# Mixture-of-experts loop of a fused graph and feed-forward kernel: the first-layer third piece loaded a step ahead in two halves, and a PSUM tile for each column half

## The chip, the core and the metric

The kernel runs on one NeuronCore of a Trainium2 chip. The metric is the device time of one execution in microseconds. The names of the engines are those of the profile: PE is TensorE (PEld its weight loads), DVE VectorE, ACT ScalarE, POOL GpSimd, SP SyncE, which in this kernel only issues transfers.

## What is computed

The program is one layer of a graph attention network over 625 nodes and 20,000 edges, followed by a transformer block with a mixture of experts. The change lies in the last part alone. In the reference that part reads:

```python
h2 = _ln(x, ln2_g, ln2_b).reshape(-1, d)                  # 625 rows of d = 768
gate_logits = h2 @ Wg                                     # 8 experts
w, sel = jax.lax.top_k(gate_logits, K)                    # K = 1
w = jax.nn.softmax(w.astype(jnp.float32), axis=-1)        # one chosen expert: weight 1
...
hid = jax.nn.relu(jnp.einsum('nd,edf->enf', h2, W1) + b1[:, None, :])   # 3072 wide
y = jnp.einsum('enf,efd->end', hid, W2) + b2[:, None, :]
moe = jnp.einsum('ne,end->nd', combine, y)
return x + moe.reshape(b, t, d)
```

With K = 1 each row goes through one expert, so the kernel sorts the rows by expert and runs each expert over its own rows only. All weights are float32. An expert has W1 of 768 x 3072 and W2 of 3072 x 768, each 9.4 MB.

## The kernel before

**Stages.** The graph layers and the attention come first. During the attention's last tiles the routing picks an expert for each row (`choose`), finds the row's place (`send`) and scatters the rows, sorted by expert, into the DRAM buffers `xg` (normed rows) and `xr` (residual rows, with the row's number in an extra column). Then the experts run.

**Steps.** A `step` takes up to 128 rows of one expert. The first one, `step_a`, takes 128 rows of the expert with the most rows; it is traced before the loop, since its expert is known early. All others run in a hardware loop (`For_i`, L1354) of as many iterations as the routing found. An expert's rows are cut into at most one block of 32, one of 64 and then blocks of 128; the loop's body holds an arm for each of the three sizes (L1370 to L1376), and a word of `table` tells the iteration its size, its expert, the next step's expert, and whether that one is new. An expert with several blocks keeps its weights.

**Weights.** An expert's weights stand in six SBUF tiles: `w1[0..2]`, each 1024 of the 3072 hidden columns of W1, and `w2[0..2]`, each 1024 of the hidden rows of W2. There is one copy of each. A piece is loaded as two transfers of 1536 KB, called halves here (`load_piece`; `load_half` is the one W2 half). `load_expert`, called behind each step, puts the next expert's loads into SP's queue in the order `w1[0]`, `w1[1]`, `w1[2]`, the second bias `b2b`, `w2[0]`, `w2[1]`, `w2[2]`; SP keeps that order (a manual schedule), and each load waits until the running step has read the tile it goes to. If the next step has the same expert, the transfers are switched off by `cond`. The last half of `w2[2]` takes another way: it is loaded into the tile `ahead` at the start of the step before (`load_ahead`, L1362), and ScalarE copies it into place at the start of its own step (L1361).

**Inside a step.** `into(c)` multiplies the rows with a block of W1 into the PSUM tile `ph`, and VectorE copies it to `hb` (L1102). `turn(c)` transposes `hb` on PE into `tp` (L1109), and ScalarE adds the first bias and applies Relu into `hbT` (L1114). `out_of(c)` multiplies `hbT` with a block of W2 and adds up in `py` (L1122), a PSUM tile with one bank for each half of the 768 columns. There are three blocks c at 32 and 64 rows, where P = 4 or 2 column groups of PE work side by side, and six at 128 rows. PE's order is written by hand; in the loop it is

```python
for c in range(2, n):
    turn(c - 2)
    into(c)
turn(n - 2)
out_of(0)
turn(n - 1)
for c in range(1, n):
    if c > n - 3:
        turned = turn_rows(xbT, xb, sp, c + 2 - n, nc.scalar.copy)
    out_of(c)
```

after `into(0)` and `into(1)`. `turn_rows` transposes the next step's rows in two parts (L892), which ScalarE copies to `xbT` (L893); its PSUM buffers are the two of `tp`. The last `out_of` does its products sorted by column half. Behind it VectorE adds the sums to `yo` in eight instructions (L1175), and POOL scatters `yo` into the output (L1177). ScalarE, VectorE and POOL have no order by hand: the planner of the framework places them.

## Time and profile before

| | |
|---|---|
| median of 3 runs | 1071.32 us (1071.0 to 1073.14) |
| the profiled execution | 1073.13 us, its span 1071.0 us |
| mean granted TensorE clock | 0.987 |
| bytes of SP's hardware queue | 175.57 MB |
| step 0 (before the loop) ends | 702.1 us |
| loop steps: rows, and start in the span | 64: 702.1; 128: 738.0; 64: 805.5; 32: 839.8; 128: 867.7; 64: 933.1; 32: 967.3; 64: 995.4; 32: 1029.7 |
| last product of the last step ends | 1057.6 us |

The profile is of one execution, and all its times are in us from the start of its span. The 2 us between its span and its own time lie outside what the trace shows. A line such as L1122 is a line of the listing above. A group "py<-ew,hbT" names the output and the inputs by tile; all of the experts' weight tiles are called `ew` there. float32 products appear as two records each. A mark in brackets at a line's end says how long the engine was idle before, and what released it. "SPq" is SP's queue: a line there is the issue of a transfer, not its duration. In the view by stretches the columns are, for each engine, busy us and (instructions), then the granted clock as a share of full speed, the busy share of the 16 DMA engines, and GB/s.

By the transfer rates in the steps, weights are fetched for the steps that start at 805.5, 839.8, 933.1, 967.3 and 1029.7; the other loop steps go on with the expert that is there.

### The profile page before, as it was taken

The numbers are of one execution on the slowest core, as the hardware profiler recorded it, in microseconds if no ns is written. First come the engines' busy times: TensorE is split into PE (matmuls) and PEld (weight loads), VectorE is DVE, ScalarE is ACT, GpSimd is POOL, SyncE is SP. The second block draws the span as 40 slices with busy tenths as digits, with TensorE's granted clock in tenths as the row PEclk, the third lists the DMA queues.
The fourth block names the chain that finished last, engine by engine and source line by source line (L and its number), as shares of the span: only waits on it lengthen the run. The fifth ranks groups of instructions, "written<-read, shape, count | busy, mean of one in ns | idle before, by whom it ended". The sixth has DMA issues, their size and how long they took to land.

```text
span 1071.0 us, 14972 instructions
## 1 busy us (share of the span) xinstructions
PE 1006.0 (94%) x4763; PEld 576.6 (54%) x4764; DVE 456.4 (43%) x1306; ACT 344.3 (32%) x826; POOL 57.1 (5%) x97
## 2 busy tenths in 40 slices
PE   6889999999999999999999999999999899997993
PEld 4455456677656556666665655544463435543341
DVE  6886696385293920665537554011101121011211
ACT  6667544362130111444435211121202222122230
POOL 1200100000000100000001102000000000000000
PEclk9999999999999999999999999999999999999997
DMA  9300400300410357998001669212798969799693
GB/s 279 135 1 1 160 30 0 133 1 17 99 32 1 83 139 171 409 390 326 1 2 42 254 234 352 88 39 98 298 321 324 400 240 347 266 379 398 241 401 130
DMA packets 85928, 194.40 MB, mean 182 GB/s; under 512 B 32413, under 2 KB 34084, under 8 KB 85865
## 3 DMA queue, kind: packets, MB, share of 16 engines
q1 hardware_dynamic: 80345, 175.57, 46.0%
q0 software_dynamic: 5440, 17.86, 4.8%
q8 instruction: 36, 0.59, 0.2%
q10 hardware_dynamic: 80, 0.16, 0.1%
q14 instruction: 27, 0.22, 0.1%
HBM read 250.30 MB, written 38.37 MB: 270 GB/s over the span
## 4 chain that ended last, share of the span: by engine, by line
PE 66%; DVE 6%; DMA 6%; issue 4%; SPq 3%; ACT 1%; POOL 1%; POOLq 0%; DVEq 0%; ACTq 0%
PE py L1122 14%; PE ph L1098 14%; PE pq L809 7%; PE agg L529 6%; DMA ew<-in_L_ffn_W_dram 6%; PE ph L591 5%; PE ph L629 3%; PE pv L772 3%; PE ph L166 3%; SPq L1030 3%; PE sc L829 2%; PE o L870 2%; PE po L901 2%; PE tpe L852 1%; PE tph L1109 1%
## 5 line engine op out<-in xcount | busy, mean ns | idle before, releaser
L1122 PE MATMUL py<-ew,hbT 128*64 128x384 f32 (+2 forms) x960 | 192.7, 503 | 14.7 <-DMA ew<-in_L_ffn_W_dram 14.7
L1098 PE MATMUL ph<-ew,xbT 128*32 128x256 f32 (+2 forms) x864 | 153.4, 497 | 8.7 <-DVE bT L1067 4.8
L1122 PEld LDWEIGHTS py<-ew,hbT 128*64 128x64 f32 (+2 forms) x960 | 92.3, 147 | 96.5 <-issue 60.4
L1114 ACT ACTIVATE hbT<-tph,bT 128x64 f32<-128x64 f32 (+2 forms) x240 | 55.5, 334 | 198.4 <-PE tph L1109 121.3
L1098 PEld LDWEIGHTS ph<-ew,xbT 128*32 128x32 f32 (+2 forms) x864 | 62.8, 135 | 88.7 <-issue 81.5
L1175 DVE TENSOR_TENSOR yo<-yo,py 64x192 f32<-64x192 f32 (+2 forms) x80 | 27.3, 378 | 182.0 <-PE py L1122 180.9
L1102 DVE COPY hb<-ph 128x512 f32<-128x512 f32 (+1 forms) x39 | 24.5, 629 | 144.5 <-PE ph L1098 144.3
L529 PE MATMUL agg<-xl,zT 125*125 125x256 f32 (+1 forms) x300 | 79.8, 417 | 1.3 <-ACT zT L518 1.1
L529 PEld LDWEIGHTS agg<-xl,zT 125*125 125x125 f32 x300 | 54.5, 188 | 19.6 <-ACT zT L518 2.6
L356 PE MATMUL pp<-w,yT 128*125 128x512 f32 x120 | 57.0, 614 | 0.0
L231 ACT ACTIVATE step<-iota,past 125x314 f16<-125x314 f16 x120 | 55.9, 547 | 0.0
L629 PE MATMUL ph<-wr,h1T 128*125 128x384 f32 x160 | 52.8, 486 | 0.0
L591 PE MATMUL ph<-w,h1T 128*125 128x384 f32 x160 | 52.4, 486 | 0.0
L838 ACT ACTIVATE e<-e,nm 125x125 f32<-125x125 f32 (+4 forms) x60 | 36.0, 602 | 39.5 <-DVE nm L835 39.4
L248 PE MATMUL cps<-step,oh 125*125 125x314 f16 x181 | 38.0, 315 | 10.5 <-ACT step L231 5.4
L901 PE MATMUL po<-wpj,aT 128*125 128x384 f32 x120 | 44.3, 499 | 1.2 <-DVE nm L835 0.7
L241 DVE TENSOR_SCALAR oh<-iota,drel,upper 125x125 f16<-125x125 f16 x160 | 41.4, 316 | 4.0 <-PE cps L248 4.0
L166 PE MATMUL ph<-wr,yT 128*125 128x512 f32 x96 | 42.1, 593 | 0.1
L591 PEld LDWEIGHTS ph<-w,h1T 128*125 128x125 f32 x160 | 30.0, 188 | 21.1 <-issue 0.5
L248 PEld LDWEIGHTS <-oh 125*125 125x125 f16 x181 | 26.1, 147 | 28.2 <-DVE oh L241 13.9
L629 PEld LDWEIGHTS ph<-wr,h1T 128*125 128x125 f32 x160 | 29.8, 188 | 20.8
L809 PE MATMUL pq<-hT,L_ffn_Wq 128*128 128x313 f32 (+1 forms) x144 | 41.0, 432 | 0.0
(331 smaller groups left out, 1281.6 us busy)
## 6 DMA issues: line engine op xcount, KB each, us to landing
ew<-in_L_ffn_W_dram SPq DMA_DIRECT2D x122, 1536.0 KB
xr<-zt SPq DMA_DIRECT2D x5, 3076.0 KB
xg<-zt SPq DMA_DIRECT2D x5, 3072.0 KB
ahead<-in_L_ffn_W_dram SPq DMA_DIRECT2D x10, 1536.0 KB
w<-in_L_gnn_W_dram SPq DMA_DIRECT2D x4, 1536.0 KB
wr<-in_L_gnn_Wr_dram SPq DMA_DIRECT2D x4, 1536.0 KB
b2b<-in_L_ffn_b_dram SPq DMA_DIRECT2D x11, 384.0 KB
xb<-xg POOLq DMA_DIRECT2D x10, 384.0 KB, 6.4
```

The costliest lines, as they stand in the source:

```text
L166: nc.tensor.matmul(pp[:R, :], yT[:, c, cols(t)], part(wr1, KD, c, i, 512), start=(c == 0), stop=(c == KD - 1))
L231: nc.scalar.activation(o, iota[:, :SH + 1], AF.Sign, bias=at, scale=-1.0)
L248: nc.tensor.matmul(where, target(R, d[:, j:j + 1], w[:, j:j + 1]), step(s[:, j:j + 1], j % 4 != 3), start=False, stop=False, skip_group_ch ...
L356: nc.tensor.matmul(pp[:R, :], yT[:, c, cols(t)], part(w1, KD, c, i, 512), start=(c == 0), stop=(c == KD - 1))
L529: nc.tensor.matmul(self.agg[:R, c0:c0 + n], zT[:, s, :], xl[:, s, x0:x0 + n], start=(s == 0), stop=(s == T - 1))
L591: nc.tensor.matmul(ph[:R, :384], h1T[:, c, cols(t)], part(w2, KH, c, i, 384), start=(c == 0), stop=(c == KH - 1))
L629: nc.tensor.matmul(ph[:R, :384], h1T[:, k, cols(t)], part(wr2, KH, k, i, 384), start=(k == 0), stop=(k == KH - 1))
L809: nc.tensor.matmul(pp[:, :b - a], w[:, c, c0:c0 + 128], hT[:, c, a:b], start=(c == 0), stop=(c == KD - 1))
L901: mm = nc.tensor.matmul(pp[:R, i, :384], aT[:, c, cols(t)], wpj[i][:, c, :], start=(c == 0), stop=(c == KD - 1))
L1098: mm = nc.tensor.matmul(ph[g * M:(g + 1) * M, :C], xT[:, k, :M], w[:, k, o + g * C:o + (g + 1) * C], start=(k == 0), stop=(k == KD - 1))
L1114: nc.scalar.activation(hbT[c][:, k, r], tp[:, k, r], AF.Relu, bias=bT[:, f:f + 1])
L1122: mm = nc.tensor.matmul(py[g * M:(g + 1) * M, i, :384], hbT[c][:, k, g * M:(g + 1) * M], w[:, o + g * K + k, i * 384:(i + 1) * 384], start ...
```

## The change

- **What is loaded ahead.** No longer the last half of `w2[2]`, but both halves of `w1[2]`. Two buffers of three 1024-column blocks hold them: `ahead[0]` takes the place of the old `ahead`, and `ahead[1]` lies in the tile `xid`, which is allocated on all 128 partitions now and whose rows are no longer needed by then. `w2[2]` is loaded whole, in its turn.
- **When.** `load_expert` in step i loads, for step i + 1, `w1[0]`, `w1[1]`, `b2b`, `w2[0]`, then `w1[2]` of step i + 2 into `ahead`, then `w2[1]` and `w2[2]`. The call before the loop still loads all three `w1` pieces. The table's words get four more bits, the expert of the step after next and whether it is new.
- **Copies.** ScalarE copies `ahead[0]` into `w1[2]` after the last `into` of a step, and `ahead[1]` after the last `turn` (in program order). The copy at a step's start is gone.
- **Sums.** `py` becomes two tiles of one bank each, `py0` and `py1`.
- **Order.** `begun` is yielded outside of the manual PE schedule.

```diff
--- before.py
+++ after.py
@@ -74,7 +74,8 @@
     xg = dram.tile([NR, D], F32, name="xg")
     xr = dram.tile([NR, D + 1], F32, name="xr")
 
-    xid = keep.tile([R, T, D + 1], F32, name="xid")
+    xid_all = keep.tile([128, T, D + 1], F32, name="xid")
+    xid = xid_all[:R]
     x = xid[:, :, :D]
     bT_all = keep.tile([128, E * NK], F32, name="bT_all")
     nc.gpsimd.iota(xid.bitcast(I32)[:, :, D:D + 1].rearrange("p t o -> p (t o)"),
@@ -1027,20 +1028,19 @@
                                        name=f"ew{l}_{c}")
 
     def load_half(to, e, c, k, **cond):
-        nc.sync.dma_start(to, W2[ds(e, 1), c * FC + k * 128:c * FC + (k + 4) * 128, :]
-                          .rearrange("o (k p) d -> p (o k) d", p=128), **cond)
+        nc.sync.dma_start(to, W1[ds(e, 1), k * 128:(k + 3) * 128, c * FC:(c + 1) * FC]
+                          .rearrange("o (k p) f -> p (o k) f", p=128), **cond)
 
     def load_piece(e, l, c, **cond):
         if l:
-
-            for k in range(0, FC // 128 - (4 if cond and c == NFC - 1 else 0), 4):
-                load_half(w2[c][:, k:k + 4, :], e, c, k, **cond)
+            for k in range(0, FC // 128, 4):
+                nc.sync.dma_start(
+                    w2[c][:, k:k + 4, :],
+                    W2[ds(e, 1), c * FC + k * 128:c * FC + (k + 4) * 128, :]
+                    .rearrange("o (k p) d -> p (o k) d", p=128), **cond)
         else:
             for k in range(0, KD, 3):
-                nc.sync.dma_start(
-                    w1[c][:, k:k + 3, :],
-                    W1[ds(e, 1), k * 128:(k + 3) * 128, c * FC:(c + 1) * FC]
-                    .rearrange("o (k p) f -> p (o k) f", p=128), **cond)
+                load_half(w1[c][:, k:k + 3, :], e, c, k, **cond)
 
     def load_bias(e, **cond):
         nc.sync.dma_start(b2b, b2[ds(e, 1), :].to_broadcast([B, D]), **cond)
@@ -1066,18 +1066,24 @@
         of_e = bT_all.rearrange("p (e k) -> p e k", k=NK)[:, ds(e, 1), :]
         return bT, nc.vector.tensor_copy(bT, of_e.rearrange("p o k -> p (o k)"))
 
-    def load_expert(e, new):
+    def load_expert(e, new, later, last=NFC - 1):
 
 
         with tc.manual_schedule(engines={SP}):
-            for l in range(2):
-                for c in range(NFC):
-                    load_piece(e, l, c, cond=new)
-                if not l:
-                    load_bias(e, cond=new)
-
-    def load_ahead(e, **cond):
-        load_half(ahead, e, NFC - 1, FC // 128 - 4, **cond)
+            for c in range(last):
+                load_piece(e, 0, c, cond=new)
+            load_bias(e, cond=new)
+            load_piece(e, 1, 0, cond=new)
+            load_ahead(*later)
+            for c in range(1, NFC):
+                load_piece(e, 1, c, cond=new)
+
+    def load_ahead(e, new=None):
+        for i in range(2):
+            load_half(ahead[i], e, NFC - 1, 3 * i, **({} if new is None else dict(cond=new)))
+
+    def from_ahead(i):
+        nc.scalar.copy(w1[NFC - 1][:, 3 * i:3 * i + 3, :], ahead[i])
 
     def step(M, xT, bT, rb, after=None):
 
@@ -1087,7 +1093,7 @@
         C = 512 if P == 1 else FC // P
         n = DF // (C * P)
         K = C // 128
-        py = sp.tile([128, 2, 512], F32, name="py", bufs=1)
+        py = [sp.tile([128, 512], F32, name=f"py{i}", bufs=1) for i in range(2)]
         hb, hbT, copied = {}, {}, []
 
         def into(c):
@@ -1120,14 +1126,15 @@
             for k, i in sorted(order, key=lambda o: o[1]) if c == n - 1 else order:
                 for g in range(P):
                     mm = nc.tensor.matmul(
-                        py[g * M:(g + 1) * M, i, :384], hbT[c][:, k, g * M:(g + 1) * M],
+                        py[i][g * M:(g + 1) * M, :384], hbT[c][:, k, g * M:(g + 1) * M],
                         w[:, o + g * K + k, i * 384:(i + 1) * 384],
                         start=(c == 0 and k == 0), stop=(c == n - 1 and k == K - 1))
             return mm
 
         with tc.manual_schedule(engines={PE}):
             into(0)
-            yield into(1)
+            begun = into(1)
+        yield begun
         if after is None:
             with tc.manual_schedule(engines={PE}):
                 turn(0)
@@ -1152,9 +1159,11 @@
                 for c in range(2, n):
                     turn(c - 2)
                     into(c)
+                from_ahead(0)
                 turn(n - 2)
                 out_of(0)
                 turn(n - 1)
+                from_ahead(1)
                 for c in range(1, n):
                     if c > n - 3:
                         turned = turn_rows(xbT, xb, sp, c + 2 - n, nc.scalar.copy)
@@ -1172,7 +1181,7 @@
             for g in range(P):
                 for cc in range(4 // P):
                     cs = slice(cc * w, (cc + 1) * w)
-                    nc.vector.tensor_add(yv[:, i, cs], yv[:, i, cs], py[g * M:(g + 1) * M, i, cs])
+                    nc.vector.tensor_add(yv[:, i, cs], yv[:, i, cs], py[i][g * M:(g + 1) * M, cs])
 
         s = nc.gpsimd.indirect_dma_start(
             out=out, out_offset=bass.IndirectOffsetOnAxis(ap=idx[:M], axis=0),
@@ -1318,6 +1327,7 @@
     w = tabf[:, 2, :NS]
     v.scalar_tensor_tensor(w, a[:, 1:], 4.0, w, op0=OP.mult, op1=OP.add)
     v.scalar_tensor_tensor(w, a[:, :NS], 64.0, w, op0=OP.mult, op1=OP.add)
+    v.scalar_tensor_tensor(w[:, :NS - 1], a[:, 2:], 1024.0, w[:, :NS - 1], op0=OP.mult, op1=OP.add)
     v.tensor_copy(table, tabf[:, 2:, :])
     rt.close()
 
@@ -1331,17 +1341,17 @@
     first_rows = nc.gpsimd.dma_start(xb, xg[ds(row_0, B), :])
     first_turned, = step_a
     right.close()
-    ahead = ctx.enter_context(tc.tile_pool(name="ahp", bufs=1, reuse_waits="tile")).tile(
-        [128, 4, D], F32, name="ahead")
+
+    ahp = ctx.enter_context(tc.tile_pool(name="ahp", bufs=1, reuse_waits="tile"))
+    ahead = [ahp.tile([128, 3, FC], F32, name="ahead"),
+             xid_all.rearrange("p t d -> p (t d)")[:, :3 * FC].rearrange("p (k f) -> p k f", k=3)]
 
     def word(i, *engines):
-        return nc.values_load(table[0:1, 0, ds(i, 1)], min_val=0, max_val=1023,
+        return nc.values_load(table[0:1, 0, ds(i, 1)], min_val=0, max_val=16383,
                               **(dict(engines=engines) if engines else {}))
 
     word_0 = word(0, SP)
-    with tc.manual_schedule(engines={SP}):
-        load_ahead((word_0 >> 7) & 7)
-    load_expert((word_0 >> 7) & 7, (word_0 >> 6) & 1)
+    load_expert((word_0 >> 7) & 7, (word_0 >> 6) & 1, ((word_0 >> 3) & 7,), NFC)
 
     def all_of(step, *of):
         with tc.manual_schedule(engines={PE}):
@@ -1353,13 +1363,11 @@
     sp_order.close()
     with tc.For_i(0, n_blk, 1, iteration_sync="reg_based") as i:
         w = word(i)
-        kind, then = w & 3, ((w >> 3) & 7, (w >> 2) & 1)
+        kind, then = w & 3, ((w >> 3) & 7, (w >> 2) & 1, ((w >> 11) & 7, (w >> 10) & 1))
         row, row_next = (nc.values_load(table[0:1, 1, ds(k, 1)], engines=[pool], min_val=0,
                                         max_val=NR - B) for k in (i, i + 1))
 
         nc.gpsimd.dma_start(xb, xg[ds(row_next, B), :])
-        nc.scalar.copy(w2[NFC - 1][:, FC // 128 - 4:, :], ahead)
-        load_ahead(then[0], cond=then[1])
         bT, s = biases((w >> 7) & 7)
         tc.add_manual_dep(s.ins, first_rows.ins.name, ORDER)
```

## The prediction

> **What bounds the kernel now.** I read the page first (busy shares, the slices), then busy time by stretch, one stretch for each step of the expert loop, then PE's timeline in one narrow step, then SyncE's queue and ScalarE in that step. The page names TensorE, and the last slices say that the DMA engines are busy too:

> ```profile
> PE 1006.0 (94%) x4763; PEld 576.6 (54%) x4764; DVE 456.4 (43%) x1306; ACT 344.3 (32%) x826; POOL 57.1 (5%) x97
> ...
> DMA  9300400300410357998001669212798969799693
> ```

> An average of 94% does not say in which stage the rest is lost. The view by stretches does. I cut the loop at its steps (starts of `yo`'s sums): 64, 128, 64, 32, 128, 64, 32, 64, 32 rows, called steps 1 to 9. The rows below are steps 3 to 7 and 9:

> ```profile
> core 0: us, PE busy (x) PEld busy (x) DVE busy (x) ACT busy (x) POOL busy (x), PEclk, DMA share, GB/s
> 805.50:839.80 34.30, 34.30 (x187) 13.50 (x186) 4.58 (x14) 8.86 (x27) 2.12 (x3) 1.00 0.92 343
> 839.80:867.70 27.90, 20.72 (x253) 10.58 (x253) 4.85 (x14) 8.21 (x27) 2.05 (x3) 0.94 0.87 336
> 867.70:933.10 65.40, 65.40 (x203) 34.78 (x202) 9.71 (x17) 10.57 (x27) 2.04 (x3) 1.00 0.83 305
> 933.10:967.30 34.20, 34.20 (x190) 13.46 (x190) 4.57 (x14) 8.86 (x27) 2.13 (x3) 1.00 0.91 343
> 967.30:995.40 28.10, 21.77 (x256) 10.30 (x254) 5.02 (x14) 8.22 (x27) 2.06 (x3) 0.94 0.86 330
> ...
> 1029.70:1057.60 27.90, 21.59 (x253) 10.00 (x252) 5.03 (x15) 8.22 (x27) 2.04 (x3) 0.94 0.85 329
> ```

> 64- and 128-row steps are full of matmuls. The three 32-row steps (4, 7, 9) are not: PE is idle 6 to 7 us in each, the granted clock drops to 0.94, and the DMA engines run through. Steps 4, 7 and 9 are the ones whose expert is loaded during a step of only 34 us. PE's timeline of step 7:

> ```profile
> 976.16 0.84 PE L1122 MATMUL py<-ew,hbT 128*32 128x384 f32 x4
> 979.40 2.89 PE L1122 MATMUL py<-ew,hbT 128*32 128x384 f32 x28 [2.41 <-DMA ew<-in_L_ffn_W_dram]
> 982.23 0.44 PE L1109 MATMUL tph<-ident,hb 128*128 128x128 f32 x2
> 982.50 0.60 PE L892 MATMUL tpx<-ident,xb 128*128 128x128 f32 x4
> 983.81 0.84 PE L1122 MATMUL py<-ew,hbT 128*32 128x384 f32 x4 [0.71 <-DMA ew<-in_L_ffn_W_dram]
> 987.74 4.46 PE L1122 MATMUL py<-ew,hbT 128*32 128x384 f32 x28 [3.09 <-DMA ew<-in_L_ffn_W_dram]
> 992.14 0.44 PE L892 MATMUL tpx<-ident,xb 128*128 128x128 f32 x2
> 992.51 2.79 PE L1122 MATMUL py<-ew,hbT 128*32 128x384 f32 x32
> ```

> The second-layer products wait for the second weights, half piece by half piece, 3.93 us apart (983.81 to 987.74: 1536 KB at 400 GB/s). An undisturbed `out_of` takes 2.79 us (last line); the one after the 3.09 us wait takes 4.46 for its last 28 matmuls alone. So the narrow step is bound by transfers, and the queue that feeds them starts here:

> ```profile
> 936.07 0.38 SPq L1030 DMA_DIRECT2D ahead<-in_L_ffn_W_dram  x1
> 937.67 14.30 SPq L1040 DMA_DIRECT2D ew<-in_L_ffn_W_dram  x6
> ...
> 956.29 18.28 SPq L1030 DMA_DIRECT2D ew<-in_L_ffn_W_dram  x5
> ```

> Twelve halves and `b2b` for step 7 go out in step 6, none before 936.07.

> **The change part by part.**

> What goes. Between 936.07 and the last landing (987.74 + 3.93 = 991.7) lie 12 halves; the change leaves 10, since the third first-layer piece has been loaded a step earlier. Step 7 without waits, added from its own starts: 967.27 to 976.16 is 8.89; then `out_of(0)` 2.79, turn and row turn 0.87, `out_of(1)` 2.79, row turn 0.37, `out_of(2)` 2.87: 18.58 us. It takes 28.1, so 9.5 is lost. Step 9 (1029.63 to 1057.60, 27.97) loses 9.4. Step 4 starts its matmuls at 844.60, 4.81 after the step before, and then takes 23.07; 1.68 of that is its first two `into` at a clock of 0.56 (7.07 against 5.39). Its weights cost 23.07 - 18.58 - 1.68 = 2.8. Together **21.7 us** hang on the weights.

> [...] This stretch follows the 3.09 us wait:

> ```profile
> 987.70:989.70 2.00, 1.96 (x17) 0.92 (x21) 0.00 (x0) 0.00 (x0) 0.00 (x0) 0.67 1.03 402
> ```

> [...] The granted clock shows the drop, so I count it as regained.

> Do the ten halves land in time? Step 6: the tail of step 6's own weights (now with two halves for step 7 ahead of them) should run to about 939.9; four halves, `b2b`, `xb` and `rb` (7.27 MB, 18.2 us) end at 958.1. The first second-layer piece can't be issued before `out_of(0)` of step 6 frees it (956.29, PE's time, unchanged). Six halves and the next rows then take 24.8: the last lands at **982.9**. Step 7 wants it at 984.0 (with the stall below): 1.1 us to spare. Step 9 has no such tail (step 8 reloads nothing): 1043.5 against 1046.4. Step 4: about 855 against 863. A late landing costs us for us in steps 7 and 9, more if the clock drops.

> What comes. The one ScalarE copy at a step's start (2.75 us) becomes two in mid-step, in all nine steps, new expert or not. In before they stand like this:

> ```profile
> 967.57 2.76 ACT L1361 COPY ew<-ahead 128x3072 f32<-128x3072 f32 x1 [5.05 <-PE py L1122]
> ...
> 976.35 1.54 ACT L1114 ACTIVATE hbT<-tph,bT 128x32 f32<-128x32 f32 x8 [1.50 <-PE tph L1109]
> ```

> At a step's start nothing urgent is queued behind the copy. In mid-step, the first copy waits for the last `into`, and behind it stand the Relus of `turn(n-2)`, for which `turn_rows` (it takes that PSUM buffer) and `out_of(1)` wait. The trace of before has no Relu held up by the copy. [...] Bounds: 0, and 2.2 where the planner also puts the second copy ahead of the last Relus; I take 1.05, since the same row gives both durations, three times: **3.1 us**. [...]

> SyncE. `load_ahead` moves behind the first second-layer piece, ahead of four halves. It waits for the second copy (about 960 in step 6), and behind it `w2[1]` waits for PE until 961.2 anyway. If that copy came only at the step's end, four halves from 968 would land by 986: 2 us late. The skipped loads of a repeated expert still walk the queue; their issue took 0.07 us. Steps 2 and 5 load 12 halves in 65 us and have room (share 0.83). The extra half before the loop lies beside step 0, where PE is full and the DMA share 0.57. POOL's transfers only see fewer bytes beside them.

> The `py` halves. The eight sums of a 32-row step take 4.62 us after the last product:

> ```profile
> 1057.60 4.62 DVE L1175 TENSOR_TENSOR yo<-yo,py 32x384 f32<-32x384 f32 x8 [13.32 <-PE py L1122]
> ```

> The last `out_of` does column half 0 first, so four sums (2.3) can begin half of 2.79 earlier. Only the last step has its sums on the chain: **1.4 us** gained; elsewhere the next step hides them. One more table instruction on VectorE: 0.09 by its twin beside it, on the chain. Leaving the manual order before `begun` lets the planner place the small routing matmuls: -1 to +1.5, taken as 0. The pauses at the first run of each arm (1.57, 2.24, 4.81; none at a repeat) stay; the bounds are 3 less and 1 more.

> Sum: 21.7 - 3.1 + 1.4 - 0.1 = **19.9 us**. The profiled execution took 1073.13 (span 1071.0), 1.8 above the median of 1071.32: 1053.2 in its terms, 1051.4 as a median.

> **The rivals.**

> New waits take a part back (16%): the last halves land 1 to 4 us late in steps 7 and 9, or copies and Relus stand in the worse order. For it: spare time of only 1.1 us. Against: even the late case above misses by 2. Twice 1 to 4, plus up to 3.5 of ScalarE: 1054 to 1063.

> No change (4%): the halves that remain are held by the release of second-layer buffers, so the last one lands as late as before. The release at 967.3 plus two halves (978) speaks against it. 1070 to 1073.

> Slower (10%): ScalarE becomes the bound in mid-step. Both copies stand ahead of the Relus on which every `out_of` waits, and PE sits through them in all nine steps: 5.5 x 9 = 49.5 against 23 gained, about 1098. It decides from 2.5 us of stall per step on average. Against it: ScalarE is busy 8 to 11 us of a step, and the wide steps have 5 us of product in between.

> As forecast (70%): 1046 to 1056.

> **How the numbers follow.** About 0.2% (2 us) is what a measurement of this kernel can tell from none. Predicted 1051.5, the likeliest case. The range 1045.5 to 1061 takes in the bounds (3.1 if no Relu is held, 3 at first runs, on the low side; late halves and copies above) and most of the first rival; the other two and its tail, 2 in 10, are outside. Faster: 0.70 + 0.16 = 0.86; same 0.04; slower 0.10.

> **What would show it.** Right: steps 7 and 9 last 19 to 21 us with no wait of `py` for `ew` over 1 us and a granted clock of 1.00; step 4 ends 1.5 to 2.5 us sooner; 64- and 128-row steps keep 34.3 and 65.4; the second-layer issues end sooner after a step starts; the last sums end about 3.2 after the last product. Wrong: `tpx` or `py` waiting over 2 us for `hbT`, 64-row steps longer than 35 us, or the waits for `ew` still at 3 us.

## The result, and the profile after

The changed kernel takes **1063.18 us** (median of 4 runs, 1062.57 to 1065.18) against 1071.16 (4 runs, 1069.79 to 1073.14): a ratio of 0.9927, 95% interval 0.9907 to 0.9948. It is faster by 5.6 to 10 us, where 20 were forecast. A second series of the same program, on another chip, gave 1061.67 and a ratio of 0.9905 (0.9885 to 0.9925). The profiled execution took 1062.57 us (span 1060.6). It is the quickest of its runs and that of before was the slowest of its own, so the two traces lie 10.4 us apart and the medians 8.

The page of the changed kernel, its row of engines:

```profile
PE 1003.9 (95%) x4763; PEld 571.8 (54%) x4764; DVE 456.6 (43%) x1307; ACT 366.6 (35%) x835; POOL 57.1 (5%) x97
```

ScalarE has 22 us more to do in nine more instructions, one copy more in each step, and PE's own sum is nearly what it was. The view by stretches, cut at the same steps as in the prediction (here 2, 4, 6, 7 and 9; same columns):

```profile
735.50:807.40 71.90, 68.06 (x200) 35.83 (x200) 7.24 (x17) 13.10 (x28) 2.08 (x3) 0.95 0.65 238
...
841.70:865.10 23.40, 19.15 (x253) 8.84 (x253) 4.99 (x13) 10.75 (x28) 2.04 (x3) 1.00 0.81 311
...
930.40:964.70 34.30, 34.30 (x191) 13.58 (x194) 5.16 (x14) 11.39 (x28) 2.13 (x3) 1.00 1.03 399
964.70:988.30 23.60, 20.58 (x254) 9.11 (x255) 5.20 (x13) 10.65 (x28) 2.05 (x3) 0.93 0.84 312
...
1022.60:1048.90 26.30, 21.52 (x252) 9.49 (x251) 5.42 (x13) 10.74 (x28) 2.05 (x3) 0.94 0.77 298
```

Step 6 keeps its 34.3 us, so the copies in mid-step hold nothing there. Step 7 falls from 28.1 to 23.6, which is far from 18.6, and its clock is still 0.93. Step 9 falls by 1.4 only, and step 4 does not fall at all. Step 2 (71.9 with its pause) has a clock of 0.95. The DMA engines carry 399 GB/s all through step 6 (busy share 1.03) and yet 311 in step 4 (0.81). PE's timeline of step 7 shows what is left of the waits:

```profile
976.99 2.79 PE L1128 MATMUL py<-ew,hbT 128*32 128x384 f32 x32
979.71 0.44 PE L893 MATMUL tpx<-ident,xb 128*128 128x128 f32 x2
980.14 0.84 PE L1128 MATMUL py<-ew,hbT 128*32 128x384 f32 x4
984.00 4.31 PE L1128 MATMUL py<-ew,hbT 128*32 128x384 f32 x28 [3.02 <-DMA ew<-in_L_ffn_W_dram]
```

The first two waits of before (2.41 and 0.71) are gone. A third of the same length is left (3.09 there), but two halves further on: in before it was for the second half of `w2[1]`, here it is for the last half of `w2[2]`. After it the 28 products take 4.31 instead of 2.8. From the two traces, step by step (start of a step's first product to that of the next), in us:

| part | before | after | difference |
|---|---|---|---|
| all up to step 1's first product | 703.59 | 701.13 | -2.5 |
| step 1, with the pause at its end | 36.56 | 38.21 | +1.7 |
| step 2 | 65.3 | 68.0 | +2.7 |
| step 3, with the pause at its end | 39.1 | 34.2 | -4.9 |
| step 4: weights +2.0, slow start -1.7 | 23.07 | 23.37 | +0.3 |
| step 7 | 28.1 | 23.6 | -4.5 |
| step 9, to its last product | 27.8 | 26.4 | -1.4 |
| after the last product | 13.55 | 11.7 | -1.9 |

Steps 5, 6 and 8 are equal within 0.1. The weights, steps 4, 7 and 9 together, gave **3.9 us of the 21.7**. A second profile of the same program divides it otherwise (step 4 lasts 25.3, step 7 23.7, step 9 24.7) but comes to nearly the same, 3.7. The rest of the difference is pauses (-2.2 with their slow starts), sums (-1.9), and work before the loop (-2.5). I don't give the last to the change: `step_a` begins at 629.15 in this trace and at 628.22 in the second series of the same program, and in all eleven profiles of this study somewhere from 628.0 to 631.2.

The new wait has its root in SP's queue in step 2, in which everything for step 3 and the `ahead` of step 4 goes out:

```profile
776.62 0.35 SPq L1046 DMA_DIRECT2D b2b<-in_L_ffn_b_dram  x1
780.68 5.97 SPq L1037 DMA_DIRECT2D ew<-in_L_ffn_W_dram  x2
787.25 0.37 SPq L1031 DMA_DIRECT2D ahead<-in_L_ffn_W_dram  x1
788.27 0.37 SPq L1031 DMA_DIRECT2D xid<-in_L_ffn_W_dram  x1
```

And busy time in stretches of 4 us there:

```profile
772.00:776.00 4.00, 4.00 (x14) 2.04 (x13) 1.02 (x3) 3.44 (x2) 0.00 (x0) 1.00 0.00 0
776.00:780.00 4.00, 4.00 (x14) 2.34 (x13) 0.60 (x1) 3.00 (x5) 0.00 (x0) 1.00 0.27 98
780.00:784.00 4.00, 4.00 (x16) 2.48 (x15) 0.00 (x0) 1.14 (x4) 0.00 (x0) 1.00 0.55 147
...
788.00:792.00 4.00, 4.00 (x14) 2.39 (x13) 0.00 (x0) 0.00 (x0) 0.00 (x0) 1.00 0.99 371
```

ScalarE's two copies out of `ahead` ended at 775.3 and 778.0, so the two `ahead` loads could have gone then. They stand behind the two halves of `w2[0]`, which wait for PE until 780.7 and 786.3, while the DMA engines have little or nothing to do. Afterwards they carry 396 GB/s from 788 to 860 (busy share 1.02), into step 4.

### The profile page after: what moved, and what is told of

The parts are those of the page before. It is cut to its first block, busy times and chain, and to the rows that moved or that the text cites. A ratio compares the mean times of both kernels' runs of the same rounds, so it can differ in the third digit from the quotient of the medians.

```text
span 1060.6 us, 15061 instructions
## 1 busy us (share of the span) xinstructions
PE 1003.9 (95%) x4763; PEld 571.8 (54%) x4764; DVE 456.6 (43%) x1307; ACT 366.6 (35%) x835; POOL 57.1 (5%) x97
## 5 line engine op out<-in xcount | busy, mean ns | idle before, releaser
L1108 DVE COPY hb<-ph 128x512 f32<-128x512 f32 (+1 forms) x39 | 24.4, 628 | 149.4 <-PE ph L1104 148.5
L836 DVE CUSTOM_DVE_ANT_0 e<-sc,later 125x125 f32<-125x125 f32 (+4 forms) x60 | 30.7, 543 | 24.1 <-PE sc L830 24.0
```

## The experiments

**Each part by itself.** First the kernel before with `py` split and nothing else, then the changed kernel with one `py`.

```diff
-        py = sp.tile([128, 2, 512], F32, name="py", bufs=1)
+        py = [sp.tile([128, 512], F32, name=f"py{i}", bufs=1) for i in range(2)]
...
-                    nc.vector.tensor_add(yv[:, i, cs], yv[:, i, cs], py[g * M:(g + 1) * M, i, cs])
+                    nc.vector.tensor_add(yv[:, i, cs], yv[:, i, cs], py[i][g * M:(g + 1) * M, cs])
```

> The kernel before with nothing changed but the two PSUM tiles py0 and py1. Theory (the change's gain lies in the transfers; the split only lets the sums of column half 0 start half an out_of earlier): the loop's steps keep their lengths (32-row steps 28 us), the tail from the last product to the end of the span falls from 13.4 to about 11.8 us, and the time falls by 1.4 to 1.7 us, to about 1069.6. Rival (the split frees PE or VectorE at each step's turn): the starts of the steps move too and 4 us or more are gained, about half of what the whole change gained.

Measured: 1067.59 us, ratio 0.9959 (0.9944 to 0.9975), 3.8 less by the medians. The loop is as long as before (354.04 us from step 1's first product to the last one, 353.86 before). The end, from the last product on, is shorter, 12.2 instead of 13.55:

```profile
1056.10:1068.30 12.20, 0.00 (x0) 0.00 (x0) 3.27 (x6) 0.00 (x0) 0.92 (x1) 0.64 0.01 3
```

Six records of VectorE in this row: the first of the eight sums (they share records) are done before the last product ends. That is about the forecast 1.4. About 1.2 more lie before `step_a`, where nothing was changed and where profiles differ anyway; what makes the rest of the 3.8, I can't say.

The reverse, the edit above undone on the changed kernel:

> The changed kernel with py as one PSUM tile of two banks again; loading ahead and the copies stay. Theory: 32-row steps as in the changed kernel (23 to 26 us), the tail back at 13.4, about 1.5 us slower than the changed kernel: 1064.7. Rival (the split is the gain): back to about 1068 to 1071.

Measured: 1064.86 us, ratio 0.9938 (0.9925 to 0.9951). That is 1.7 above the first series of the changed kernel and 3.2 above the second, which runs on different chips can hardly tell apart: its ratio's interval overlaps that of the first series. The trace is clearer. From the last product to the end it has 13.4 us again, against 11.7 in the changed kernel.

**Less to transfer.** The changed kernel with the third second-layer piece not loaded again in the loop, so that `w2[2]` keeps the values of the first expert. It leaves two of twelve halves out of each new expert, and keeps all copies and products.

```diff
-            for c in range(1, NFC):
+            for c in range(1, NFC - 1):
                 load_piece(e, 1, c, cond=new)
```

> The changed kernel without the reloads of w2[2] in the loop: from the second expert on, the third second-layer piece is left as it was (so the last out_of of those experts multiplies the first expert's weights). 10 halves of 12 are moved for an expert. Theory (what is left of the 32-row steps' waits is bytes: the DMA engines run without a pause from the end of the wide step on): the waits for ew vanish, steps 4, 7 and 9 last 18.6 to 20 us instead of 23.4, 23.6 and 26.3, and the time is 1046 to 1050. Rival (the two ScalarE copies hold Relus and row copies, and PE waits for them): the 32-row steps stay at 22 us or more, with waits of tpx or py for ScalarE, and the time is above 1056.

Measured: 1047.85 us, ratio 0.979 (0.9768 to 0.9812). Steps 4, 7 and 9:

```profile
841.60:859.70 18.10, 18.10 (x254) 8.49 (x253) 4.82 (x12) 10.68 (x28) 2.05 (x3) 1.00 0.61 221
...
959.30:977.60 18.30, 18.22 (x256) 8.56 (x254) 4.97 (x13) 10.67 (x28) 2.05 (x3) 1.00 0.60 214
...
1011.80:1030.00 18.20, 18.20 (x254) 8.51 (x252) 4.87 (x12) 10.67 (x28) 2.05 (x3) 1.00 0.56 215
```

No idle time, the clock at 1.00, ScalarE with both copies in each step: 18.1 to 18.3 us, even under the 18.58 that I had added up for a step without waits. So the whole of what the changed kernel still loses in its narrow steps is transfers, and ScalarE's copies cost nothing that these steps show.

**The `ahead` loads one place earlier.** The same bytes and copies; in SP's queue the two loads stand in front of `w2[0]`.

```diff
             load_bias(e, cond=new)
-            load_piece(e, 1, 0, cond=new)
             load_ahead(*later)
+            load_piece(e, 1, 0, cond=new)
```

> The changed kernel with the two loads into ahead put in front of w2[0] in SyncE's queue instead of behind it. Theory (the loads ahead stand too far back: in steps 2 and 5 they go out at 787 and 910 although their buffers are free at 778 and 901 and the DMA engines are idle there): they start about 8 us earlier, the second-layer halves behind them are no longer pushed into the next step, the last landing for steps 4 and 7 comes 6 to 8 us earlier, these two steps fall to about 20 us, step 9 gains 1 to 5 us, and the time is about 1054 (1051 to 1057). Rival (the number of bytes binds, whatever their order): the same 24 halves for steps 3 and 4 end at the same time, 1062 to 1064.

Measured: 1051.08 us, ratio **0.9816** (0.9796 to 0.9835). Repeated on another chip, to be compared with the GpSimd run below:

> The kernel with the loads into ahead in front of w2[0] once more, on the chip of the run with POOL's queue and for a second profile. Both theories: 1050 to 1054, the 32-row steps at 19 to 22 us.

It gave 1052.27 and 0.9817 (0.9795 to 0.9838). In the trace of the first, stretches of 4 us in step 2 and then steps 4, 7 and 9:

```profile
766.00:770.00 4.00, 4.00 (x14) 1.98 (x13) 0.63 (x2) 3.05 (x2) 0.00 (x0) 1.00 0.00 0
770.00:774.00 4.00, 4.00 (x14) 2.40 (x13) 0.99 (x3) 3.39 (x5) 0.00 (x0) 1.00 0.34 116
774.00:778.00 4.00, 4.00 (x16) 2.48 (x15) 0.00 (x0) 1.14 (x4) 0.00 (x0) 1.00 0.96 364
...
841.00:860.80 19.80, 19.80 (x252) 11.56 (x252) 3.22 (x7) 10.65 (x28) 1.08 (x2) 0.91 0.82 304
...
960.40:980.70 20.30, 19.17 (x256) 8.85 (x254) 4.92 (x13) 10.65 (x28) 2.05 (x3) 1.00 0.88 330
...
1014.90:1036.40 21.50, 19.10 (x254) 8.82 (x252) 4.97 (x13) 10.64 (x28) 2.04 (x3) 1.00 0.85 325
```

The transfers set in right behind the copies (issue at 771.97 and 772.98), and the DMA engines' busy share is 0.96 from 774 on, which in the changed kernel it reaches at 788 (0.99). Steps 4, 7 and 9 are 3.6, 3.3 and 4.8 us shorter than in the changed kernel, and 19.8 in step 4 still holds 1.7 of slow clock, after a pause of 4.87 that this program has there (at step 2 it has a shorter one). This version beats both kernels, before by 18.5 to 20 us and the changed one by 9 to 12.

The profile of the repetition is of its slowest run (1055.23). Steps 4 and 7 last 20.9 and 20.3 there, but step 9 24.9, more than expected: it waits 3.01 us and has a slow clock behind it. So the gain in step 9 is not the same in every execution.

**The changed kernel again**, on the chip of the next two runs.

> The changed kernel once more, beside the two below, and for a second profile of it. Both theories: 1062 to 1065. If the pause at the first 128-row step (5.3 us in PE's branch, 732.1) belongs to the program's layout, it is there again, and none at the first 32-row step; if it is chance, it stands elsewhere. The part ahead of the first expert step differs by up to 3 us between the profiles so far; if that is chance, it is not at 629.1 again.

1061.67, as told above, just under the forecast. Step 9 lasts 24.6 instead of 26.4 here and step 4 25.3 instead of 23.4. The pause in front of step 2 is 3.83 again, and none is in front of step 4. `step_a` begins at 628.22, so that start differs between executions of one program.

**What held step 9.** Steps 7 and 9 of the version above keep waits of 1.02 and 2.39 us. In the changed kernel, SP's queue from the end of step 7 into step 8:

```profile
983.99 0.07 SPq L1046 DMA_DIRECT2D b2b<-in_L_ffn_b_dram  x1
986.09 0.38 SPq L1031 DMA_DIRECT2D ahead<-in_L_ffn_W_dram  x1
987.10 0.38 SPq L1031 DMA_DIRECT2D xid<-in_L_ffn_W_dram  x1
...
996.43 4.09 SPq L1031 DMA_DIRECT2D ew<-in_L_ffn_W_dram  x4
```

Step 8 has the expert of step 7, so `b2b` is a skipped load with nothing to wait for. Yet it passes at 983.99, when the last half of `w2[2]` lands (PE's release is 984.00), and `ahead` for step 9 goes behind it, though its copies were done in mid-step. Next the first `w1` of step 8's call passes at 996.43, when the load into `xid` lands. SP's view of waits names it (us in all, times, largest):

```profile
SPq L1031 <- DMA xid<-in_L_ffn_W_dram: 7.5, 2, 4.1
```

The trace's record of each issue names the semaphore that the transfer's completion counts up. The thirteen transfers of an iteration use eight, 140 to 147, in turn, and each iteration starts again with 140. So 140 to 144 serve two transfers of an iteration each. In before and in the changed kernel none of the loop's transfers passes before the one that last used its semaphore has landed, skipped ones among them, as far as landings are recorded, and 26 pass 0.1 to 0.4 us behind that landing: `b2b`, the fifth, waits for the thirteenth of the iteration before, the last half of `w2[2]` (landed at 983.86), and the first half of `w1[0]` waits for the ninth, the load into `xid` (landed at 996.29). To shift the partners, I added three transfers of 64 bytes to spare tiles (sixteen to an iteration; the lines that allocate the tiles are left out here) and put `ahead` in front of `b2b`:

```diff
+            load_ahead(*later)
             load_bias(e, cond=new)
-            load_ahead(*later)
             load_piece(e, 1, 0, cond=new)
+            for i in range(3):
+                nc.sync.dma_start(spare[i], b2[0:1, 0:16])
```

> The loads into ahead in front of b2b and w2[0], and three transfers of 64 bytes into spare tiles between w2[0] and w2[1], so that SyncE has 16 transfers in an iteration instead of 13. Theory (a transfer can be issued only when the one that last used its completion semaphore has landed; with 8 semaphores in turn and 13 transfers, b2b and all behind it in step 7 wait for the last w2[2] half of that step, 977.96 there): with 16 in turn the loads into ahead wait for w2[1] only, go out when ScalarE's second copy is done (about 3 us before the last landing of step 7), and run on without a pause behind it; step 8's w1 is 2 to 3 us earlier, the 2.39 us wait in step 9 falls below 0.5, and the time is 1 to 2.5 us less than with ahead in front alone (1051.1), 1048.5 to 1050. Rival (the order in the queue alone counts): no gain over it, or a loss by the three extra transfers, 1051 to 1052.

Measured: 1055.99 us (1051.17 to 1061.54), ratio 0.9852 (0.9822 to 0.9881): not the gain I expected. By the medians it is 4 us worse than without, but its runs spread over 10 us and the intervals of the two ratios overlap, so what is shown is that nothing was gained. SP's queue, steps 7 and 8:

```profile
970.82 0.39 SPq L1031 DMA_DIRECT2D ahead<-in_L_ffn_W_dram  x1
976.81 0.38 SPq L1031 DMA_DIRECT2D xid<-in_L_ffn_W_dram  x1
...
990.75 3.48 SPq L1031 DMA_DIRECT2D ew<-in_L_ffn_W_dram  x4
```

And stretches of 5 us:

```profile
980.00:985.00 5.00, 5.00 (x34) 1.75 (x28) 4.39 (x8) 0.00 (x0) 0.00 (x0) 1.00 1.02 409
985.00:990.00 5.00, 5.00 (x26) 1.58 (x23) 0.88 (x2) 0.00 (x0) 1.49 (x2) 1.00 0.15 43
```

The mechanism is there: `ahead` for step 9 goes out in mid-step 7. But the skipped issues of `w2[1]` now have `ahead`'s landings as their partners, and the `w1` for step 9 comes at 990.75, after 5 us of almost idle engines. Step 9 took 26.5 with waits of 0.77 and 3.04. One wait was traded for another of the same kind.

**The pauses.** PE stops before the first run of an arm, for 4.81 us at step 4 of before. The trace has it in the branch itself. PE's sequencer in before, in the changed kernel (two lines), and below in a version with the arms tested in another order (times: number, then min/median/max in ns, then from and to):

```profile
L1373 PEldq COMPARE_BRANCH  x2: 214/3042/5871, 836.4 to 844.1; - x2
```

```profile
L1381 PEldq COMPARE_BRANCH  x1: 5310/5310/5310, 732.1 to 732.1; - x1
L1381 PEldq COMPARE_BRANCH  x2: 194/204/214, 838.3 to 840.3; - x2
```

A branch in the loop takes at most 0.4 us, or at an arm's first run 3.2 to 6.0. In the changed kernel step 4 has no such branch, but the one for step 2 takes 5.31, and it did so again in the second series.

What moves meanwhile stands in the view of the transfers. Beside the data it lists a queue named "instruction". In before, during the branch in front of step 4 (`--dma --window 836.4:842.3`):

```profile
q8 instruction: 1, 0.02, 1.2%
```

This packet of 16 KB moves from 839.94 to 841.05, and the branch ends 1.2 us later. The loops of before and of the changed kernel have five long branches of PE, 3.4 to 5.9 us. Each has exactly one such packet inside it and ends 1.2 to 1.4 us after the packet does. During the short ones, at most 0.4 us each, none moves but in one of 59: before's branch at 739.70, 1.6 us after a long one, while the next packet (739.40 to 740.78) was under way. What the packet holds the traces do not show; the queue's name is all that I have for taking it as a piece of the program's own code.

To see whether the pauses hang on where the arms lie, `ahead` in front of `w2[0]` (not shown again) and the tests turned round (32, 64, 128 rows):

```diff
-        with tc.If(kind == 0) as cmp:
-            part(B)
+        with tc.If(kind == 2) as cmp:
+            part(32)
...
-                part(32)
+                part(B)
```

> The kernel with the loads into ahead in front of w2[0], and the loop's arms tested in the order 32, 64, 128 rows. Theory (the pauses of 3 to 6 us at the first run of an arm are PE's branch to code that hasn't been fetched, so they go with the place of the arm's code): the pauses move; the 32-row arm, now next to the loop's head, starts at step 4 without the 4.9 us pause, and the 128-row arm, now last, pauses at step 2, where no weights are moving. Time 1048 to 1054. Rival (a pause belongs to the step, whose transfers or tables are late): step 4 pauses for 4.9 us as before and the time is 1051.

Measured: 1055.39 us (1051.66 to 1063.44), ratio 0.9869 (0.9831 to 0.9907). Its branches at step 2 and at step 4:

```profile
L1381 PEldq COMPARE_BRANCH  x2: 214/1746/3279, 731.9 to 737.0; - x2
L1381 PEldq COMPARE_BRANCH  x1: 194/194/194, 833.9 to 833.9; - x1
```

The pause at step 4 (4.87 us in the version it is built on) is gone. The branch at step 2 is as long as it was there (3.21), so no pause has moved to it. The changed kernel and the version below have no pause at step 4 either, with the arms in their old order: the order alone doesn't decide. The time is above the forecast and no better. Step 4 comes earlier, its transfers don't, and PE waits 1.86 us for them with a granted clock of 0.50 behind, so that steps 3 and 4 together gain 2.2; step 9 waits 3.04. A pause in front of a step that waits for transfers is time in which transfers run. Its runs also spread over 12 us, which I can't explain.

**Another queue.** The `ahead` loads, in front of `w2[0]` again, issued by GpSimd, so that nothing in SP's order can hold them. Not shown are the new parameter `by` of `load_half` and the table's word that GpSimd reads too.

```diff
-            load_half(ahead[i], e, NFC - 1, 3 * i, **({} if new is None else dict(cond=new)))
+            load_half(ahead[i], e, NFC - 1, 3 * i, by=nc.gpsimd, **({} if new is None else dict(cond=new)))
```

> The kernel with the loads into ahead in front, but issued by POOL from its own queue (behind rb, in front of the scatter of yo), so that they wait for ScalarE's copies alone and SyncE has 11 transfers in an iteration. Theory (in step 7 these loads are held by the transfers in front of them in SyncE's queue, and SyncE in turn by them; free of each other, step 8's w1 goes out when PE releases it, 2.6 to 3.5 us after the step's start, instead of 6 to 8): step 9's wait for ew falls below 1 us and the step to about 19 us; step 7 may lose up to 3 us, since the first of the two loads shares the DMA engines with its last halves. Time 1047 to 1052. Rival (bytes alone: whatever order the halves go in, the last one for step 9 lands at the same time): step 9 at 21.5 us or more, step 7 longer too, 1052 to 1056.

Measured: 1059.0 us, ratio 0.989 (0.9872 to 0.9908), above both forecasts. Steps 4 and 9:

```profile
836.80:864.10 27.30, 20.75 (x255) 9.20 (x253) 5.22 (x13) 10.77 (x28) 3.61 (x5) 0.94 0.92 356
...
1021.50:1041.30 19.80, 19.11 (x254) 8.81 (x252) 5.01 (x13) 10.67 (x28) 2.19 (x5) 1.00 0.83 318
```

Step 9 is the shortest of all versions with all their bytes, as expected. I had overlooked the other side: freed from the order, the `ahead` for a later step shares the DMA engines with the last halves that the running step still waits for (5.13 us in step 4, and 3.19 in step 7). The 5.13 is not all due to that, since no pause precedes step 4 here; but none does in the version with the turned arms, and there the same half let PE go 52.5 us after the start of step 3, here 57.2. SP's order, which delays `ahead`, also protects these halves.

## Why the prediction was wrong

**The step that failed** is "Do the ten halves land in time?". It put the last landing at 982.9 in before's time, 15.6 us after the start of step 7, at 13.9 after that of step 9, and for step 4 at 49.5 after that of step 3. PE was released 19.4, 21.9 and 54.9 us after these starts, 3.8, 8.0 and 5.4 later than forecast. Its spare times had been 1.1, 2.9 and 8. In steps 4 and 9 of the changed kernel:

```profile
862.29 2.77 PE L1128 MATMUL py<-ew,hbT 128*32 128x384 f32 x28 [2.82 <-DMA ew<-in_L_ffn_W_dram]
1044.44 4.47 PE L1128 MATMUL py<-ew,hbT 128*32 128x384 f32 x28 [2.88 <-DMA ew<-in_L_ffn_W_dram]
```

Step 4 is a case of its own. With the pause of 4.81 us in front of it, which the forecast kept, even this landing would have been in time (863 is 57.5 after the start of step 3). The pause went, and PE came that much sooner.

The first thing missing is the place of the prefetch in the queue. I asked whether `load_ahead`, moved behind `w2[0]`, would hold up what stands behind it, and found that `w2[1]` waits for PE anyway. I did not ask what stands before it. In step 2 it went out at 787 where it could have gone at 778, and the bytes behind it came later: the last half of `w2[2]` for step 3 landed 11.0 us after that step's start, and 7.7 in the version with `ahead` in front. From 788 to 860 the DMA engines carry 17 halves with bias, rows and scatters; at the 396 GB/s of this stretch its 72 us are 28.5 MB, of which the halves are 26.7. For step 7 the sum let the tail of step 6's own weights end 6.9 us after the start of step 6. Its last half landed 11.5 after it, and these 4.6 us more than cover the 3.8. In the version with `ahead` in front it landed 7.1 after it, close to the 6.9.

The second is the end of such a burst, which the sum took as sharp. Here it ran out over 2.2 us. In the last 2 us in front of the release at 862.29:

```profile
860.00:861.00 1.00, 0.00 (x0) 0.00 (x0) 0.00 (x0) 0.00 (x0) 0.00 (x0) 1.00 0.25 98
861.00:862.00 1.00, 0.00 (x0) 0.00 (x0) 0.00 (x0) 0.00 (x0) 0.00 (x0) 1.00 0.06 25
```

The first of the sixteen shares of that half landed at 859.96, the last at 862.15.

The third is the semaphores that transfers share. They held the `ahead` for step 9 until 986 and its first `w1` until 996.43, 8.2 us after the start of step 8, where step 6 had needed 3.4: 4.8 of the 8.0 in step 9. I had counted a skipped load as 0.07 us of issue. The trace of before already shows that such loads wait, in SP's view of waits from 700 to 1060:

```profile
SPq L1040 <- DMA ew<-in_L_ffn_W_dram: 32.9, 11, 4.5
```

The rows for the next step suffered too. Their load, issued at 847.14 in step 4, landed 7.7 us later among the halves (fifteen of its sixteen shares after 6.1), and PE's row turn waited 1.43. The view names the Relus as what released it, but they were done at 853.3, and the rows landed at 854.85.

The size of what the halves can give was right. In the version with less to transfer steps 4, 7 and 9 are 24.4 us shorter than in before, 1.7 of it the slow start of step 4. With `ahead` one place earlier they are 17.4 shorter in the first profile and 13.0 in the second. That this version's 1051.08 and 1052.27 are the time that I had forecast for the change is partly luck: 3.4 and 2.5 us of its gain lie ahead of the loop, and the 3.1 for ScalarE were not lost.

**ScalarE**: forecast +3.1, measured about 0 (steps of 18.1 to 18.3 without late weights). I had let the copy begin behind the last `into`. It only overwrites the part of `w1[2]` that the first three blocks k have read, so it begins earlier; ScalarE in step 7 of the changed kernel:

```profile
972.09 2.75 ACT L1086 COPY ew<-ahead 128x3072 f32<-128x3072 f32 x1
974.74 1.53 ACT L1120 ACTIVATE hbT<-tph,bT 128x32 f32<-128x32 f32 x8
```

The last `into` ends at 973.08, a us after the copy's start, and the Relus behind it are done at 976.27, just before PE comes to `turn_rows` at 976.43, for which they free the buffer. So the Relus do stand behind the copy in this step (they begin 2.65 us after it) and hold nobody. The 3.1 of the sum was my estimate of PE standing 1.05 us in each narrow step for Relus behind the copy, and the 3.5 of ScalarE in the first rival and the spare times of 1.1 and 2.9 rest on it too. No run shows it: the three narrow steps without late weights have 0.08 us of idle PE at most. The term was wrong in its starting point.

**`py` halves**: forecast -1.4 and +0.1, measured -1.9 after the last product here and -1.4 in the kernel with that part alone. The sums in the changed kernel:

```profile
1046.59 1.71 DVE L1184 TENSOR_TENSOR yo<-yo,py 32x384 f32<-32x384 f32 x3 [10.60 <-PE py L1128]
...
1048.96 2.88 DVE L1184 TENSOR_TENSOR yo<-yo,py 32x384 f32<-32x384 f32 x5 [0.67 <-PE py L1128]
```

Three sums lie beside the last products, five behind them: 2.9 us instead of 4.62, as forecast.

**Pauses**: taken as 0 with bounds of 3 less and 1 more; measured -2.2. The one in front of step 4 went (4.81) and with it the slow start behind it (1.68); the one before step 2 grew from 2.24 to 3.89. Its larger price is behind the pause:

```profile
739.34 13.24 PE L1104 MATMUL ph<-ew,xbT 128*128 128x512 f32 x24 [3.89 <-DVE bT L1067]
```

24 products take 13.24 us here, 10.54 before.

**The clock**: I counted the products that were slow behind a wait as regained, and the runs stand by that (a clock of 1.00 in steps 4, 7 and 9 of the version with less to transfer), but a wait's length is not what decides. Waits of 2.88 and 3.02 in the changed kernel slowed the next 28 products to 4.47 and 4.31, one of 2.82 did not (2.77). Yet one of 1.86 did so in the version with the turned arms (4.47), and one of 3.59 in the version with one `py` left the clock alone (its step 2 takes 62.3 us between PE's branches at 737.7 and 800.0, before's 62.4, the changed kernel's 65.1). The clock records show a difference between these waits. In before and in the changed kernel all changes of the granted clock lie whole multiples of 3.413 us apart. I cut both executions at such points. From 600 us on the clock fell from 1.00 to 0.50 behind the eight stretches in which PE had stood idle for 2.52 to 3.09 us, and behind no other; the idlest of the others had 1.82. In the version with the turned arms the 1.86 us lie in one stretch:

```profile
852.60:856.01 3.41, 1.55 (x14) 0.48 (x16) 0.00 (x0) 1.58 (x3) 0.00 (x0) 1.00 0.47 184
856.01:859.42 3.41, 3.41 (x24) 1.30 (x16) 1.64 (x3) 0.00 (x0) 0.00 (x0) 0.50 0.61 175
```

In the version with one `py` the 3.59 us, in front of step 2, are split between two, 1.74 and 1.85:

```profile
732.87:736.28 3.41, 1.67 (x12) 0.47 (x8) 1.60 (x6) 0.00 (x0) 0.00 (x0) 1.00 0.33 127
736.28:739.70 3.42, 1.57 (x4) 0.87 (x5) 1.06 (x4) 0.00 (x0) 0.97 (x1) 1.00 0.02 5
```

So in these four executions it mattered how much of a wait lay in one such stretch of 3.41 us: 1.86 slowed the clock, 1.85 did not. One reading of mine was off: over the 7.07 us of the first two `into` of step 4 in before the clock is 0.76, not 0.56, which leaves the 1.68 as it was.

**The rivals.** "New waits take a part back" is what came, with the mechanism that it named first, late halves in steps 7 and 9. Its 1054 to 1063 was just too narrow, because it allowed 1 to 4 us where 3.8 and 8.0 came, and had step 4 safe. Why they would be late, the order and the shared semaphores, it did not name. "No change" and "Slower" did not come: second-layer buffers were free in time, and ScalarE's queue held nobody.

What stays open: the 2 us more than its shorter end that the split of `py` gave by itself; why the pause, and the packet with it, comes at one arm in one program and at another in the next; and the 1 to 3 us by which the part before the loop differs from profile to profile.

## What to carry to other kernels

When a transfer is moved ahead in time, look up what stands before it in its queue as well as behind it, and find the stretch in which the DMA engines are idle: here the two `ahead` loads of step 2 went out at 787 where they could have gone at 778, and the version with them in front was 9 to 12 us faster. Count for a deadline all that shares the engines, scatters, rows and the end of a burst (2.2 us here) included, ask what a skipped transfer still waits for, and doubt a sum whose spare time is smaller than what it leaves out. A second queue was no remedy by itself: with it step 4 waited 5.13 us, and the order in one queue had also kept later goods from the way of urgent ones.
